# A graph-convolution and expert kernel: edge masks inside the degree stage, first chunk counted behind the degrees, h made two tiles at a time

## The chip, the cores and the metric

The kernel runs on one core of a Trainium2 chip. The metric is the device time of one execution in microseconds; runs of one kernel are compared by their median. Five engines work in parallel, each through its own instructions in order: TensorE (PE: matmuls, with weight loads shown as PEld), VectorE (DVE), ScalarE (ACT), GpSimd (POOL) and SyncE (SP), which only issues DMAs here. They wait for each other through semaphores.

## The reference, cut to what matters

The inputs are 6250 nodes with 256 features each and 200000 edges, `src[e]` to `dst[e]`, sorted by `dst`. The part in question is the graph convolution:

```python
deg_out = clip(segment_sum(ones, src), 1.0)
deg_in  = clip(segment_sum(ones, dst), 1.0)
h = feats * rsqrt(deg_out)[:, None]
m = segment_sum(h[src], dst) * rsqrt(deg_in)[:, None]
x = m @ W_gc + b_gc + (feats @ W_res + b_res)
```

Behind it come a top-2 mixture of 64 experts (`x @ Wg`, the two best experts of each node, a two-layer network per expert with GELU), a normalisation over the nodes, the sum with the input, and a layer norm over the features. The change touches none of these.

## The kernel before

The nodes lie in 50 tiles (`NT`) of 125. The edges lie in 1563 groups of 128, one edge per partition, one group per column of `dst` and `src` (padded to 1568 columns, `NGR`).

**Degree stage (lines 412 to 456).** A loop over 49 steps `i`, of 32 groups each (`CG`). In each step VectorE builds two one-hot tensors of `src`: `hot_hi` (its tile number, 50 values) and `hot_lo` (its place in the tile, 128 values), both at line 243. TensorE multiplies them group by group and so counts the out-degrees in `degp` (line 436). In the same step TensorE turns one tile of the features (line 383) and multiplies it by the two weight matrices (`project`, line 392); ScalarE copies the result (`hx`, line 396), and SyncE's queue carries one half to `r_dram` and the other into `hrow`, the rows of h in SBUF. From step 8 on GpSimd makes one `ind` tensor per step (line 428) that TensorE multiplies (`held`), and ScalarE makes the masks `mis` (line 456): for each group, how far each edge's `dst` lies from the start of its window.

**The gap behind it (lines 460 to 544).** VectorE sums the degrees, ScalarE takes the square root, VectorE the reciprocal (`s_out`). Then come the halves of h: each tile of `hrow` is scaled and split into a rounded half (ScalarE, line 488) and the remainder to it (line 491 on VectorE; for every third tile ScalarE makes the product `whole` and GpSimd subtracts, line 496). Every four or six tiles go to `h_dram` by SyncE's queue. Calls of `halves(0)` to `halves(40)`, ten tiles each, alternate with VectorE's mask steps: which edges of the first 1025 groups (`GD`) fit their window, which key each of them has (`key`, in f32), how many do not fit (`nmis`, `some`, `redo`), and a table `mf` of the edges left over, which GpSimd completes and writes to `mis_dram`.

**Aggregation (lines 551 to 827).** The first 1025 groups are "dense": 31 chunks, each a window of 128 destination nodes. For each group VectorE makes a one-hot `hotk` from `key` (line 615; every eighth group also `lo`, line 243), TensorE counts edges between source places and windows (line 625), and ScalarE copies the counts of one slot into `counts` (line 633), of which there are two, for even and odd chunks. Then `multiply(c, t)` multiplies the counts of chunk `c` by tile `t` of `hrow`, in two halves (lines 640 and 641), for 50 tiles. Chunk 0 has 20 slots of two groups, 40 counts. The counts of chunk `c + 1` lie between the tiles of chunk `c`; chunk 1 has 57 slots, 114 counts. `hot_of` runs seven groups ahead (`KB`). Before chunk 0 is counted, ScalarE clears `counts[0]` (five steps, line 595); it clears `counts[1]` between the counts of chunk 0. The remaining 538 groups are "gathered": GpSimd fetches the 128 source rows of a group from `h_dram` by an indirect DMA (line 567, a ring of six) and TensorE multiplies them by a one-hot of the window (lines 572 and 573).

The order of all this is written out by hand (`manual_schedule`): a generator `dense()` yields each piece of work with planned microseconds, and a gather is put in whenever the planned time passes `LEAD + n * every`, where `every` is chosen so that the last gather comes 5 planned microseconds before the end. The planned times are no durations; they only set the order. The plan gives 11.9 to the counting of chunk 0 and reaches 50.6 at its last tile.

Behind the aggregation come routing and the experts, unchanged.

## Time and profile before

| | us |
|---|---|
| median of three runs | 1770.24 (1765.89 to 1771.05) |
| the profiled execution | 1785.41 |
| its span | 1783.6 |
| TensorE busy in it | 1468.9 (82%) |
| VectorE busy | 1005.9 (56%) |
| GpSimd busy | 936.1 (52%) |
| ScalarE busy | 700.6 (39%) |
| mean granted TensorE clock | 0.929 of full speed |

The profile is one execution. Its times count from the start of its span. "Line, engine, operation, out<-in, shape, xcount" names an instruction or a merged run of equal ones; behind it in the timeline stands, in brackets, how long the engine was idle before and what released it; in a list of groups stand the busy time, the mean duration in ns, and the idle time before. A row by stretches gives the length, the busy time of TensorE, its weight loads, VectorE, ScalarE and GpSimd with their instruction counts, the granted clock, the DMA engines' busy share and the rate in GB/s. Starts and ends of matmuls are modelled in part, and a few of their records are missing. The degree stage lies between about 30 and 186 us, the aggregation between 227 and 1087, the experts behind 1180.

### The profile page before, as it was taken

The page shows a single profiled execution, that of the slowest core. Times are in us where ns is not written, and L with a number is a line of the kernel's source. Part 1 is how long each engine was busy: PE and PEld are TensorE (multiplying, and loading weights), DVE is VectorE, ACT ScalarE, POOL GpSimd, SP SyncE. Part 2 cuts the span into 40 slices and gives each one's busy share as a digit, 9 for nine tenths or more (in the row PEclk, how much of TensorE's full clock was granted, in tenths as well). Part 3 has the DMA queues.
Part 4 walks back from the last instruction along what each step waited for, and adds up shares of the span by engine and source line. Part 5 has one row for each costly group of instructions (what it writes and reads, how often), then busy time and mean ns, then how long its engine had stood idle before and what let it go on. Part 6 is the DMA issues. An engine that isn't in the chain of part 4 may idle for free. (4 is left out here: it accounts for less than half of the span.)

```text
span 1783.6 us, 31676 instructions
## 1 busy us (share of the span) xinstructions
PE 1468.9 (82%) x10293; PEld 1220.2 (68%) x10293; DVE 1005.9 (56%) x2588; ACT 700.6 (39%) x1703; POOL 936.1 (52%) x984
## 2 busy tenths in 40 slices
PE   5999168788899998999898896359999999999740
PEld 3555057677788888888888795248878887777520
DVE  8999886676666565545454551862322322221796
ACT  2333663333455554445444441032222222222248
POOL 3562436666666666666666664025655666554000
PEclk8999668999999999999999998579999999999875
DMA  5898766676777777677776773917878888675834
GB/s 169 245 257 243 237 179 180 194 196 190 206 214 195 199 213 209 186 211 205 201 206 199 215 205 109 223 48 225 265 221 246 251 248 255 202 252 183 222 88 127
DMA packets 221105, 362.19 MB, mean 203 GB/s; under 512 B 24820, under 2 KB 149614, under 8 KB 220930
## 3 DMA queue, kind: packets, MB, share of 16 engines
q1 hardware_dynamic: 158039, 180.12, 35.0%
q0 software_dynamic: 55328, 172.48, 34.4%
q10 hardware_dynamic: 7562, 7.47, 1.5%
q8 instruction: 84, 1.38, 0.3%
q14 instruction: 92, 0.75, 0.2%
HBM read 279.11 MB, written 74.47 MB: 198 GB/s over the span
## 5 line engine op out<-in xcount | busy, mean ns | idle before, releaser
L567 POOL DMA_INDIRECT r<-h_dram,srcg x538 | 556.6, 1035 | 301.5 <-issue 112.5
L640 PE MATMUL sm<-hrow,counts 125*128 125x258 f32 x1550 | 504.3, 341 | 8.6 <-issue 6.0
L633 ACT CAST counts<-pc 128x300 f32 (+7 forms) x804 | 356.3, 443 | 328.4 <-PE pc L625 160.3
L615 DVE TENSOR_SCALAR hotk<-iota_h,key 128x300 bf16<-128x300 f16 (+7 forms) x1025 | 274.2, 307 | 329.4 <-PE pc L625 169.3
L641 PE MATMUL sm<-hrow,counts 125*128 125x256 f32 x1550 | 418.9, 285 | 1.1 <-issue 1.1
L640 PEld LDWEIGHTS sm<-hrow,counts 125*128 125x128 f32 x1550 | 305.5, 197 | 76.1 <-issue 67.6
L625 PE MATMUL pc<-hotk,lo 128*128 128x300 bf16 (+7 forms) x1025 | 281.7, 302 | 85.6 <-issue 39.3
L641 PEld LDWEIGHTS sm<-hrow,counts 125*128 125x128 f32 x1550 | 302.3, 195 | 1.6 <-issue 1.0
L1262 ACT ACTIVATE hT<-ph,b1c 128x128 f32<-128x128 f32 (+8 forms) x256 | 109.2, 438 | 350.3 <-PE ph L1260 224.6
L1272 PE MATMUL py<-w2s,hT 128*128 128x256 f32 (+3 forms) x992 | 239.5, 384 | 4.6 <-issue 3.1
L1260 PE MATMUL ph<-xgT,w1s 128*128 128x128 f32 (+8 forms) x1024 | 211.8, 351 | 8.3 <-ACT hT L1262 4.1
L1260 PEld LDWEIGHTS ph<-xgT,w1s 128*128 128x128 f32 x1024 | 171.2, 193 | 41.7 <-issue 16.4
L1272 PEld LDWEIGHTS py<-w2s,hT 128*128 128x128 f32 (+3 forms) x992 | 165.4, 175 | 46.0 <-issue 7.8
L572 PE MATMUL pg<-r,hot 128*128 128x258 f32 x538 | 178.4, 332 | 19.1 <-issue 8.4
L1226 POOL DMA_INDIRECT y_dram<-ys,dest x124 | 119.2, 961 | 134.0 <-DVE ys L1275 63.1
L1226 POOL DMA_INDIRECT xg<-x_dram,ids x124 | 121.3, 978 | 110.6 <-DVE ids L1178 70.5
L573 PE MATMUL pg<-r,hot 128*128 128x256 f32 x538 | 152.9, 284 | 0.0
L1275 DVE TENSOR_TENSOR ys<-py,b2s 128x256 f32<-128x256 f32 (+3 forms) x124 | 51.7, 421 | 179.0 <-PE py L1272 118.8
L625 PEld LDWEIGHTS <-lo 128*128 128x128 bf16 x1025 | 90.0, 102 | 72.4 <-issue 26.3
L572 PEld LDWEIGHTS pg<-r,hot 128*128 128x128 f32 x538 | 104.7, 195 | 36.1 <-issue 17.9
L1250 DVE COPY xgT<-pte 128x256 f32<-128x256 f32 (+7 forms) x64 | 38.5, 601 | 160.9 <-PE pte L1248 69.9
L573 PEld LDWEIGHTS pg<-r,hot 128*128 128x128 f32 x538 | 104.4, 194 | 1.2 <-issue 0.4
(317 smaller groups left out, 1826.3 us busy)
## 6 DMA issues: line engine op xcount, KB each, us to landing
w1s<-in_L_gnn_w_dram SPq DMA_DIRECT2D x64, 512.0 KB
w2s<-in_L_gnn_w_dram SPq DMA_DIRECT2D x64, 512.0 KB
y_dram<-zeros SPq DMA_DIRECT2D x48, 256.0 KB
yr<-y_dram SPq DMA_DIRECT2D x25, 448.0 KB
r<-h_dram,srcg POOLq DMA_INDIRECT x538
b2s<-in_L_gnn_b_dram SPq DMA_DIRECT2D x64, 128.0 KB
h_dram<-hrow SPq DMA_DIRECT2D x5, 1344.0 KB
z_dram<-zeros ACTq DMA_DIRECT2D x7, 903.0 KB
```

Source lines behind the costliest of these rows:

```text
L567: G.indirect_dma_start(out=f32(r[:, :2 * D]), out_offset=None, in_=h_dram[:, :], in_offset=bass.IndirectOffsetOnAxis(ap=idx, axis=0))
L572: T.matmul(pg, hot, r[:, D:], start=first, stop=False)
L573: T.matmul(pg[:, :D], hot, r[:, :D], start=False, stop=last)
L615: V.tensor_scalar(hots[g], iota_h[:, :NT * w], key[:, g:g + 1], None, op0=ALU.is_equal)
L625: T.matmul(pc, los[g // PAIRS][:, r // 2, :, r % 2], hots.pop(g), start=(i == 0), stop=(i == k - 1))
L633: S.copy(counts[c % 2][:, :, ds(live["at"][j % 8], w)], pc.rearrange("p (t w) -> p t w", w=w))
L640: T.matmul(sm, by, hrow[:, t, D:], start=(t == 0), stop=False)
L641: T.matmul(sm[:, :D], by, hrow[:, t, :D], start=False, stop=(t == NT - 1))
L1226: w = G.indirect_dma_start(**kw)
L1260: T.matmul(ph[:, :m], w1s[:, kk, c * 128:(c + 1) * 128], xgT[:, kk, :m], start=(kk == 0), stop=(kk == 1))
L1262: S.activation(hT[:, c, :m], ph[:, :m], AF.Gelu, bias=b1_e[:, c:c + 1])
L1272: T.matmul(py[:n], hT[:, c, k * 128:k * 128 + n], w2s[:, c, :], start=(c == 0), stop=(c == 3))
```

## The change

The masks of the dense groups are made with fewer steps and inside the degree loop, at fixed steps `i` (the table `masks`): the difference to the window's start, that difference clipped, "clipped differs from unclipped" as the mark of an edge that does not fit, and the key. `wide` now holds the width less one for the clip, and is then overwritten by ScalarE with the tile number times the width. For the gathered groups ScalarE writes the distance straight into `keyg`, and two VectorE steps make their mask. ScalarE sums both marks with `accum_out`, and makes `mf` apart from its last sum, which GpSimd does at step 41 (`FIRST_IND + ND + 1`); the write of `mis_dram` follows at step 42. The `ind` tensors start at step 9. `away` gets a third row, one small VectorE step. A one-column square root at step 46 precedes the real one.

Behind the degrees, the first one-hots and the counts of chunk 0 follow at once. `halves(t)` now makes two tiles, `t - 1` and `t`: two rounded halves on ScalarE, the product of the second tile on VectorE, its subtraction on GpSimd, the remainder of the first on VectorE. One such pair follows every four counts of chunk 0 (ten pairs), the other fifteen come before every second tile of chunk 0's multiplication. The six first fetches and the first one-hots of the gathers (`first_rows`) follow the last pair; the sums over the misfits (`left_edges`) come at tile 45. `counts[1]` is filled with zeros by a DMA from the cleared `z_dram` on ScalarE's queue. `LEAD` goes from 30 to 50. The SBUF pools are put in another order, so that what is used last in the degree stage lies under what is used late in the aggregation.

```diff
-LEAD = 30.0
+LEAD = 50.0
...
+            following = lp.tile([128, NGR], F32, name="following", tag="dst")
+            hi = lp.tile([128, NGR], F32, name="hi", tag="b")
+            zeros = lp.tile([128, D + 2], F32, name="zeros")
+            unfit = lp.tile([128, GD], FP16, name="unfit")
+            fit = lp.tile([128, NGR - GD], FP16, name="fit")
+            kd = dp.tile([128, GD], FP16, name="kd")
+            kc = dp.tile([128, GD], FP16, name="kc")
+            past = dp.tile([128, NGR - GD], FP16, name="past")
...
-                    G.memset(wide[:, DENSE[a][0]:g0 + k * n], float(w))
+                    G.memset(wide[:, DENSE[a][0]:g0 + k * n], float(w - 1))
+                    wides.append((DENSE[a][0], g0 + k * n, w))
...
+            CG, FIRST_IND = 32, 9
...
+            masks = {
+                8: lambda: V.tensor_tensor(kd, dstf[:, :GD], key[:, :GD], ALU.subtract),
+                10: lambda: V.scalar_tensor_tensor(kc, kd, 0.0, upmost, op0=ALU.max, op1=ALU.min),
+                12: lambda: V.tensor_tensor(unfit, kc, kd, ALU.not_equal),
+                14: lambda: V.scalar_tensor_tensor(kd, unfit, -4096.0, kc, op0=ALU.mult, op1=ALU.add),
+                16: lambda: V.tensor_tensor(key[:, :GD], kd, wide, ALU.add),
+                18: lambda: S.activation(kd, unfit, AF.Copy, accum_out=nmis[:, 0:1]),
+                19: lambda: S.activation(mf[:, :GD], unfit, AF.Copy, scale=-4.0 * FAR, bias=4.0 * FAR),
+                25: lambda: V.tensor_scalar(past, keyg, 0.0, None, op0=ALU.is_ge),
+                26: lambda: V.scalar_tensor_tensor(fit, keyg, float(WIN), past, op0=ALU.is_lt, op1=ALU.mult),
+                28: lambda: S.activation(past, fit, AF.Copy, accum_out=nmis[:, 1:2]),
+                29: lambda: S.activation(mf[:, GD:], fit, AF.Copy, scale=FAR),
+                FIRST_IND + ND + 1: lambda: G.tensor_tensor(mf, mf, dstf, ALU.add),
+                FIRST_IND + ND + 2: lambda: G.dma_start(out=mis_dram, in_=mf),
+            }
+            off = [(S.activation, (keyg[:, g0 - GD:g0 - GD + k], dstf[:, g0:g0 + k], AF.Identity),
+                    neg[:, ND + c:ND + c + 1]) for c, (g0, k) in enumerate(GATHER)]
...
-                    V.scalar_tensor_tensor(upmost, following[:, :GD], 1.0, wide, op0=ALU.add, op1=ALU.min)
+                    V.scalar_tensor_tensor(upmost, following[:, :GD], 0.0, wide, op0=ALU.add, op1=ALU.min)
+                    for g, h, w in wides:
+                        S.activation(wide[:, g:h], hi_b[:, g:h], AF.Copy, scale=float(w))
...
-                if i >= 8:
-                    c = i - 8
+                if i in masks:
+                    masks[i]()
+                if i >= FIRST_IND:
+                    c = i - FIRST_IND
...
+                if i == 7:
+                    S.activation(keyg[:, NGU - GD:], dstf[:, NGU:], AF.Copy)
+                if i == 46:
+                    dsb = dp.tile([128, D], F32, name="dsb", tag="some")[:, :128]
+                    V.memset(dsb, 0.0)
+                    S.activation(kd[:, :1], ones[:, :1], AF.Sqrt)
...
-            V.tensor_tensor(kd, dstf[:, :GD], key[:, :GD], ALU.subtract)
...
-            S.activation(s_out, s_out, AF.Sqrt)
-            V.tensor_scalar(fit, mis, 0.0, None, op0=ALU.is_ge)
-            V.tensor_scalar(t1, mis, float(WIN), None, op0=ALU.is_lt)
-            V.reciprocal(s_out, s_out)
-
...
-            halves(0)
-            fd, td, wd = fit[:, :GD], t1[:, :GD], dp.tile([128, GD], FP16, name="wd")
-            V.tensor_mul(fit, fit, t1)
-            V.tensor_scalar(td, kd, 0.0, None, op0=ALU.is_ge)
-            V.tensor_mul(fd, fd, td)
-            V.tensor_tensor(wd, kd, upmost, ALU.subtract)
-            V.tensor_scalar(td, wd, 0.0, None, op0=ALU.is_lt)
-            halves(10)
-            V.tensor_mul(fd, fd, td)
-
-            V.scalar_tensor_tensor(t1, dstf, float(N), fit, op0=ALU.is_lt, op1=ALU.subtract)
-            mf = dp.tile([128, NGR], F32, name="mf", tag="b")
-            G.tensor_scalar(mf[:, :GD], t1[:, :GD], -4.0 * FAR, 4.0 * FAR, op0=ALU.mult, op1=ALU.add)
-            G.tensor_scalar(mf[:, GD:], t1[:, GD:], -FAR, FAR, op0=ALU.mult, op1=ALU.add)
-            G.tensor_tensor(mf, mf, dstf, ALU.add)
-            G.dma_start(out=mis_dram, in_=mf)
-            nmis = dp.tile([128, 1], F32, name="nmis")
-            V.tensor_reduce(nmis, t1, AX.X, ALU.max)
...
-            V.tensor_mul(wd, wide, hi_b[:, :GD])
-            V.tensor_add(kd, kd, wd)
-            V.tensor_scalar(kd, kd, BIG, None, op0=ALU.add)
-            halves(30)
-            V.tensor_mul(kd, kd, fd)
-            V.tensor_scalar(key[:, :GD], kd, BIG, None, op0=ALU.subtract)
-
-            V.tensor_copy(keyg, mis[:, GD:])
-            pn = ps_a.tile([1, 128], F32, name="pn", tag="pt")
-            T.transpose(pn, nmis, ident)
...
+            nc.scalar.dma_start(out=f32(counts[1]).rearrange("p t w -> p (t w)"),
+                                in_=z_dram[0:25 * 128, :].rearrange("(p r) d -> p (r d)", p=128)[:, :NT * WIN])
+            cleared(0, 0, 10)
+            cleared(0, 10, 10)
+            S.activation(s_out, s_out, AF.Sqrt)
+            for t0 in range(20, NT, 10):
                 cleared(0, t0, 10)
+
+            wholes = [t[:, u, :D] for t in (xs.tile([TP, 2, D + 2], F32, name="whole", tag="z"),
+                                            xs.tile([TP, 2, D], F32, name="whole2", tag="xr2")) for u in range(2)]
+
+            def halves(t):
+                for u in (t - 1, t):
+                    S.activation(hrow[:, u, :D], f32(hrow[:, u, D:2 * D]), AF.Copy, scale=s_out[:, u:u + 1])
+                whole = wholes[t // 2 % 4]
+                V.tensor_scalar(whole, f32(hrow[:, t, D:2 * D]), s_out[:, t:t + 1], None, op0=ALU.mult)
+                G.tensor_tensor(hrow[:, t, D:2 * D], whole, f32(hrow[:, t, :D]), ALU.subtract)
+                V.scalar_tensor_tensor(hrow[:, t - 1, D:2 * D], f32(hrow[:, t - 1, D:2 * D]), s_out[:, t - 1:t],
+                                       f32(hrow[:, t - 1, :D]), op0=ALU.mult, op1=ALU.subtract)
+                if t % 5 == 4 or t % 10 == 5:
+                    n = 6 if t % 10 == 5 else 4
+                    node_dma(nc.sync, False, f32(hrow[:, t + 1 - n:t + 1, :2 * D]), node_rows(h_dram, t + 1 - n, n))
+
+            def left_edges():
+
+                V.tensor_sub(nmis[:, 0:1], nmis[:, 0:1], nmis[:, 1:2])
...
-                    if c == 0 and j % 4 == 3 and j < 20:
-                        cleared(1, j // 4 * 10, 10)
...
+                V.reciprocal(s_out, s_out)
                 g, n = 0, DENSE[0][1] * DENSE[0][3]
+                made_of = 1
                 for g in range(n):
                     yield of_one_hots(0) / n, lambda g=g: count(g)
+                    if g % 4 == 3:
+                        yield 0.0, lambda t=made_of: halves(t)
+                        made_of += 2
...
+                        if c == 0 and t % 2 == 0 and made_of < NT:
+                            yield 0.0, lambda t=made_of: halves(t)
+                            made_of += 2
+                            if made_of > NT:
+                                yield 0.0, lambda: first_rows()
+                        if c == 0 and t == 45:
+                            yield 0.0, lambda: left_edges()
...
-            for n in range(NR):
-                fetch(ring[n], srcg[:, rows[n][1] - GD:rows[n][1] - GD + 1])
-            hot_rows(0)
+            def first_rows():
+                for n in range(NR):
+                    fetch(ring[n], srcg[:, rows[n][1] - GD:rows[n][1] - GD + 1])
+                hot_rows(0)
```

79 lines of the change are left out of this document (28 added, 51 removed).

## The prediction

> **What bounds the kernel now.** I read the page, then busy time stretch by stretch around the change, the waits, the timeline. The first count, first and last multiplication of chunk 0, and first gather are picked from TensorE's timeline; the stretches are cut there.
>
> ```profile
> 56.00:152.00 96.00, 96.00 (x1141) 56.58 (x1143) 94.26 (x62) 36.89 (x118) 62.96 (x29) 1.00 0.87 251
> 185.70:227.60 41.90, 0.40 (x2) 0.13 (x3) 37.05 (x64) 32.88 (x74) 20.31 (x33) 0.54 0.82 254
> 227.60:240.50 12.90, 6.23 (x40) 3.55 (x40) 10.91 (x52) 11.41 (x27) 0.00 (x0) 0.50 0.90 282
> 240.50:262.00 21.50, 19.22 (x135) 16.61 (x136) 18.02 (x78) 11.87 (x37) 9.10 (x8) 0.78 0.33 87
> 262.00:283.30 21.30, 17.16 (x111) 14.63 (x111) 14.30 (x56) 6.86 (x22) 14.47 (x14) 0.78 0.66 185
> 283.30:1077.70 794.40, 711.45 (x5255) 645.20 (x5255) 455.84 (x1510) 374.62 (x861) 529.35 (x513) 0.99 0.73 201
> 240.55 0.58 PE L640 MATMUL sm<-hrow,counts 125*128 125x258 f32 x1 [1.89 <-ACT counts L633]
> 283.27 0.42 PE L641 MATMUL sm<-hrow,counts 125*128 125x256 f32 x1
> ```
>
> Columns: stretch, length, then busy time of TensorE, its weight loads, VectorE, ScalarE, GpSimd; then the clock, DMA share and GB/s. In the degree stage (first row) TensorE and VectorE are both full. Then TensorE stands still for 41.9 us while VectorE (37.05) makes masks and halves of h. Counting chunk 0 takes 12.9 more. From 283.3 on TensorE is 90% busy (711.45 of 794.40), so its work sets the pace there. What the change can win lies between 180 and 283.3.
>
> **The change, part by part.** First, the masks that move into the degree loop.
>
> ```profile
> 106.61 1.11 PE L436 MATMUL degp<-hot_lo,hot_hi 128*50 128x128 bf16 x32
> 107.78 0.98 DVE L243 TENSOR_TENSOR hot_hi<-hi_b,iota 128x1600 bf16<-128x1600 bf16 x1
> 108.68 2.37 DVE L243 TENSOR_TENSOR hot_lo<-lo_b,iota 128x4096 bf16<-128x4096 bf16 x1
> 113.07 1.11 PE L436 MATMUL degp<-hot_lo,hot_hi 128*50 128x128 bf16 x32
> 151.85 0.21 DVE L371 CAST places<-pp 31x64 int32<-31x64 f32 x1 [1.68 <-PE pp L370]
> 177.88 2.27 DVE L243 TENSOR_TENSOR hot_lo<-lo_t,iota 128x4096 bf16<-128x4096 bf16 x1
> 180.74 1.11 PE L436 MATMUL degp<-hot_lo,hot_hi 128*50 128x128 bf16 x32
> 182.51 1.23 DVE L470 TENSOR_TENSOR kd<-dstf,key 128x1025 f16<-128x1025 f32 x1
> L480 DVE TENSOR_SCALAR fit<-mis 128x1568 f16<-128x1568 f16 x1 | 0.6, 559 | 0.0
> L505 DVE TENSOR_TENSOR fit<-fit,t 128x1025 f16<-128x1025 f16 x1 | 0.7, 697 | 0.0
> L511 DVE SCALAR_TENSOR_TENSOR t<-dstf,fit 128x1568 f16<-128x1568 f32 x1 | 1.8, 1793 | 0.0
> ```
>
> VectorE gets seven mask steps in the loop. The difference and the final key go through f32: 1.23 each, 2.46. Two fused steps over 1025 columns cost 1.79 x 1025/1568 = 1.17 each, 2.34; one over 543 columns 0.62. `not_equal` on 16-bit data 0.70 (the L505 row; 1.23 if it ran like kd). `is_ge` over 543 columns 0.3 (under the 0.56 for 1568). With one small step for `away` (0.2, like L371), 6.6 us.
>
> How much of this shows? VectorE issues hot_hi and hot_lo back to back, and hot_hi starts as the degree matmul two steps earlier ends (107.72 and 107.78): both engines are tight. VectorE's 1.68 us wait at L371 shrinks by about 1.0 when it is the later engine, and its lead over TensorE at the end (180.15 to 180.74) gives 0.6. So 5.0 remain. The whole lead inside the loop (the hot_lo that ends at 111.05 is used at 113.07, so 2.0) could be absorbed instead of the 0.6; then it is 3.6.
>
> Beside this, GpSimd's sum of mf moves from the gap to step 41 of the loop.
>
> ```profile
> 205.82 3.48 POOL L515 TENSOR_TENSOR mf<-mf,dstf 128x1568 f32<-128x1568 f32 x1
> 206.11 3.23 DVE L521 TENSOR_SCALAR okc<-okc,okd 128x31 f32<-128x31 f32 x1
> 214.94 0.84 POOL L496 TENSOR_TENSOR hrow<-whole,hrow 125x256 fp32r<-125x256 f32 x1 [0.20 <-ACT whole L495]
> 215.33 1.01 DVE L526 TENSOR_TENSOR kd<-kd,wd 128x1025 f16<-128x1025 f16 x1
> L491 DVE SCALAR_TENSOR_TENSOR hrow<-hrow,s_out 125x256 fp32r<-125x256 f32 x33 | 17.8, 595 | 2.4 <-ACT hrow L488 2.4
> L496 POOL TENSOR_TENSOR hrow<-whole,hrow 125x256 fp32r<-125x256 f32 x17 | 14.2, 836 | 51.7 <-ACT whole L495 50.4 <-DMA h_dram<-hrow 1.2
> 223.58 3.13 DVE L491 SCALAR_TENSOR_TENSOR hrow<-hrow,s_out 125x256 fp32r<-125x256 f32 x7
> ```
>
> A 31-column step of VectorE (L521) lasted 3.23 us and ended with GpSimd's L515: it was held. L526 (1.01 against 0.70 for L505) also ends one ordinary duration after GpSimd's 0.84 us subtraction. In the loop VectorE has only such 16-bit two-input steps, so mf costs 0 to 3.3; I take 3.0, by the L521 row. The degree stage thus ends 8.0 us later (3.6 to 9.9).
>
> Behind the degrees ScalarE is on the path.
>
> ```profile
> 164.78 0.43 ACTq L452 DMA_DIRECT2D z_dram<-zeros  x1
> 185.62 0.59 ACT L396 COPY hx<-pr 125x512 f32<-125x512 f32 x1 [1.13 <-PE pr L392]
> L479 ACT ACTIVATE s_out<-s_out 125x50 f32<-125x50 f32 x1 | 0.2, 245 | 0.0
> 223.70 3.59 ACT L595 ACTIVATE counts<-iota_f 128x1280 fp32r<-128x1280 f32 x3 [0.45 <-issue]
> 229.64 1.17 ACT L633 CAST counts<-pc 128x100 f32 x4
> L488 ACT ACTIVATE hrow<-hrow,s_out 125x256 fp32r<-125x256 f32 x50 | 21.6, 496 | 0.5 <-DVE s_out L482 0.5
> ```
>
> On the old time axis: hx done 186.2, one DMA issue 0.43, five clears of counts[0] at 1.20, Sqrt 0.24: 192.9. Two count copies at 0.29 and one half of h at 0.43 (21.6/50) later, at 193.9, VectorE has its first difference to make, done by 194.4. VectorE's seven first one-hots, and TensorE's first counts, lie before that.
>
> ```profile
> 17.54 0.91 DVE L154 TENSOR_SCALAR hi<-hi 128x1440 f32<-128x1440 f32 x1
> 229.69 1.32 DVE L615 TENSOR_SCALAR hotk<-iota_h,key 128x100 bf16<-128x100 f16 x8
> 270.16 1.68 DVE L615 TENSOR_SCALAR hotk<-iota_h,key 128x150 bf16<-128x150 f16 x8
> L243 DVE TENSOR_TENSOR lo<-lo_b,iota 128x1024 bf16<-128x1024 bf16 x9 | 6.1, 675 | 0.0
> 258.01 0.36 PE L572 MATMUL pg<-r,hot 128*128 128x258 f32 x1
> 258.33 0.24 PE L625 MATMUL pc<-hotk,lo 128*128 128x150 bf16 x1
> 192.25 45.15 SPq L165 DMA_DIRECT2D h_dram<-hrow  x20
> ```
>
> A round is four counts and one pair of tiles. VectorE: four one-hots at 0.165 (0.66), half a `lo` (0.34), and the pair. The pair is one product (0.27: between 0.16, scaled from L154, and 0.45), one fused step (3.13/7 = 0.45), and what GpSimd's subtraction takes from VectorE. For that: nothing in the 3.13 row, (17.8 - 33 x 0.45)/17 = 0.17 over all fused steps, 0.3 for L526, up to 0.84 if the whole operation were serial. I take 0.28, next to L526, since most steps here are of its kind: pair 1.0, round 2.0. ScalarE needs only 1.45 per round. Nine more rounds end at 212.4. So chunk 0 can be multiplied some 20 us earlier on the gap's side (240.5 against 212.4 + 8.0).
>
> Then 15 pairs remain, beside chunk 1's counts: until tile 28 VectorE makes 76 one-hots at 0.21 (16.0), 9.5 `lo` (6.4) and the pairs (15.0): 37.4, to 249.8. The last 21 tiles: 38 one-hots and five `lo`, 11.4, then seven tiles at some 0.43: 14.4; the old stretch 262 to 283.3, less eleven gathers at 0.32 (258.01 to 258.33), gives 17. I take 15: 264.8, with the 8.0 of the degree stage 272.8, against 283.5.
>
> That wins 10.7. But 18 gathers that ran before 283.3 (counted in the timeline) now come after: with LEAD 50 the plan starts them at the end of chunk 0. At 0.32 on a full TensorE, 5.8. **Sum: 4.9 us faster.**
>
> Costed at nothing: chunk 1's clearing by DMA (3.3 MB, 12 us at the 282 GB/s of the counting row; needed only after tile 1, some 25 us after its issue on ScalarE's queue; that queue's earlier writes are long out); late, it would hold the counts' copies. The ScalarE sums in the loop (ScalarE is 36.89 of 96 busy, and 31 small mask steps leave it). The mis_dram write, now on GpSimd's queue inside the loop (784 KB, 3 us of transfers, with the DMA at 0.87). `left_edges`: ten tiny steps at tile 45, where VectorE has no one-hots left; TensorE's transpose may wait 0.5. The six fetches, now behind the last pair on GpSimd's queue: h written by about 262 (pairs done at 257.8, plus a tenth of the 45.15 us), ten us before the first gather; without this cover they would hold that gather. SP's queue only gets the same h writes earlier.
>
> The profiled execution took 1785.41 us, its span 1783.6; the median of the runs is 1770.24, 0.85% less. 1785.4 - 4.9 = 1780.5, times 1770.24/1785.41: 1765.4 as a median.
>
> **The rivals.** *VectorE and GpSimd shut each other out* (the other side). If each subtraction costs VectorE its full 0.84, a pair is 1.56, and 24 pairs on the path add 13.4: 8.5 slower, 1778.7. It decides above a pair of 1.2. L521 and L526 speak for it, the 3.13 row (a subtraction ran under it) against. The Trainium skill (SBUF — State Buffer, "SBUF: two separate sides") states just this: VectorE's 2-port modes, or two SBUF inputs against a GpSimd operation that reads SBUF, hold one port pair exclusively. By that rule the time would be 1779; L521 agrees with it, the fused steps do not.
>
> *The cover is better*: the loop absorbs the masks (3.6 instead of 8.0, with mf in VectorE's gaps as the ind steps are: hot_lo 2.37 against 2.27) and pairs cost 0.72. Then 4.4 + 6.7 more: 16 us faster, 1754.5. The h write bounds it: 45 us of transfers cannot start before 197.
>
> *The counting does not move*:
>
> ```profile
> PE pc L625 <- DMA h_dram<-hrow: 17.6, 1, 17.6
> ```
>
> The first count is listed as released by a write of h. Were that real, only the 8.0 would remain: 1778. But VectorE's one-hot, its last pair of steps behind the halves, ends just before it; the wait reads better as VectorE's.
>
> **How the numbers follow.** About 0.3% (5.3 us) is what can be told from no change. Chances: forecast, 0 to 10 us faster, 0.45 (0.25 of it beyond 0.3%); better cover 0.20; port 0.25 (0.05 within 0.3%); no move or another wait 0.10 (0.03 within). Faster 0.45, same 0.28, slower 0.27. The range 1750 to 1780 takes in the better cover and the port case at its price; the forecast's own is 1760 to 1770.
>
> **What would show it.** Last degree matmul near 189 instead of 180.7; VectorE without idle from step 10 on; a long hot step of VectorE beside mf. First count near 195, the gap under 10 us. Chunk 0's first multiplication near 220, last near 273, no gather before it. VectorE over 90% busy from 200 to 258, a pair's steps near 1.0. From then on the same pace, some 0.6 gathers more per chunk. Wrong if: a pair costs over 1.2, the loop grows over 10, TensorE waits for counts[1] or for h, or the clock stays at half beyond chunk 0.

## The result, and the profile after

The changed kernel takes 1788.44 us (1783.80 to 1791.39) where the kernel before, run beside it, takes 1770.64 (1765.89 to 1773.54): a ratio of 1.0101, 95% interval 1.0068 to 1.0134. It is 17.8 us slower; 4.9 us faster was forecast, and the range ended at 1780.

The two profiles do not show this in their spans (1783.6 before, 1782.0 after): that of before comes from an execution 15 us above its median, that of after from the fastest one of its kernel. Chips differ too: the kernel before takes 1784, 1768 and 1664 us on three of those used below. So the pages are read here for the order of things, and times are compared only between runs on one chip. A trace is one execution too, and can lie some us above or below the median of its kernel; where that matters, it is said.

First, stretches of the changed kernel (degree stage, the gap before the first count, counting, chunk 0, the rest of the dense chunks), and last the rest in the kernel before. The end of chunk 0 and of the rest is the last matmul of the 50th tile of chunk 0 and of chunk 30, found by counting the multiplications. Columns as in the prediction: stretch, length, busy time of TensorE, its weight loads, VectorE, ScalarE, GpSimd, clock, DMA share, GB/s.

```profile
56.00:160.00 104.00, 99.60 (x1170) 58.70 (x1169) 100.11 (x66) 34.84 (x96) 88.90 (x30) 0.97 0.81 234
191.31:196.81 5.50, 3.83 (x10) 1.60 (x11) 3.03 (x14) 2.19 (x3) 0.00 (x0) 1.00 0.88 248
196.81:220.74 23.93, 7.47 (x41) 2.91 (x41) 19.28 (x68) 16.37 (x45) 6.46 (x21) 0.57 0.72 249
220.74:271.49 50.75, 41.30 (x219) 32.94 (x219) 49.51 (x177) 29.34 (x89) 19.22 (x22) 0.57 0.72 220
271.49:1096.88 825.39, 731.21 (x5401) 660.58 (x5400) 462.14 (x1530) 375.48 (x865) 544.69 (x534) 0.99 0.72 203
284.97:1098.59 813.62, 727.38 (x5366) 659.93 (x5364) 458.56 (x1524) 375.83 (x864) 532.03 (x515) 0.99 0.72 199
```

TensorE's timeline of the same kernel: the last degree matmul, the first count, the first multiplication, the first gather, the last multiplication of chunk 0.

```profile
190.17 1.12 PE L466 MATMUL degp<-hot_lo,hot_hi 128*50 128x128 bf16 x32
196.81 1.08 PE L625 MATMUL pc<-hotk,lo 128*128 128x100 bf16 x7 [1.68 <-issue]
220.74 0.58 PE L638 MATMUL sm<-hrow,counts 125*128 125x258 f32 x1 [2.66 <-ACT counts L633]
270.59 0.30 PE L535 MATMUL pg<-r,hot 128*128 128x258 f32 x1
271.21 0.28 PE L639 MATMUL sm<-hrow,counts 125*128 125x256 f32 x1
```

From the end of the last degree matmul to the first count it takes 5.5 us (191.29 to 196.81), where the kernel before took 45.7 (181.85 to 227.58; the prediction's 41.9 begins 4 us later, behind the last matmul of the degree sums). Up to here all is as forecast: first multiplication 220.74 (forecast 220.4), end of chunk 0 271.5 (272.8). In the kernel before chunk 0 ends at 285.0: the 283.27 that the prediction shows as its last multiplication is three tiles earlier, and its stretch up to 1077.7 ends 21 us ahead of the last multiplication of the dense chunks. Chunk 0 is thus done 13.5 us earlier than before. Then 825.4 us follow where the kernel before took 813.6, in an execution 15 us above its median. The loss lies there, where the change moves little but the places of the gathers.

What starts later is GpSimd's stream of fetches. The kernel before, from the timelines of SyncE and GpSimd: the writes of h (first issue, length from first to last), the first, seventh and last of the 538 fetches.

```profile
192.25 45.15 SPq L165 DMA_DIRECT2D h_dram<-hrow  x20
244.55 1.13 POOL L567 DMA_INDIRECT r<-h_dram,srcg  x1 [20.13 <-issue]
258.76 1.75 POOL L567 DMA_INDIRECT r<-h_dram,srcg  x1 [6.28 <-PE pc L625]
1081.49 1.01 POOL L567 DMA_INDIRECT r<-h_dram,srcg  x1 [0.49 <-PE sm L659]
```

The changed kernel, the same four:

```profile
210.87 48.52 SPq L165 DMA_DIRECT2D h_dram<-hrow  x20
264.71 1.27 POOL L530 DMA_INDIRECT r<-h_dram,srcg  x1 [6.16 <-DMA h_dram<-hrow]
273.20 0.95 POOL L530 DMA_INDIRECT r<-h_dram,srcg  x1 [0.30 <-issue]
1083.58 1.01 POOL L530 DMA_INDIRECT r<-h_dram,srcg  x1 [1.91 <-remote]
```

The first fetch comes 20.2 us later: the degree stage ends 9.4 later (180.74 to 190.17), from there to the first write of h it takes 9.2 more (11.5 to 20.7, since clears, counts and rounds of pairs now lie between), the writes take 3.4 longer, and the rest takes 1.8 less (7.1 to 5.3 from the last write's issue to the fetch). In the kernel before, the seventh fetch waited 6.28 us for the first gather to free a buffer of the ring; in the changed one nothing waits, so the seventh is 14.4 us later. This is the place to look.

### The profile page after: what moved, and what is told of

It reads as the page before. It is cut to its first block, busy times and chain, and to the rows that moved or that the text cites. A ratio compares the mean times of both kernels' runs of the same rounds, so it can differ in the third digit from the quotient of the medians.

```text
span 1782.0 us, 31709 instructions
## 1 busy us (share of the span) xinstructions
PE 1482.6 (83%) x10293; PEld 1222.6 (69%) x10293; DVE 1000.0 (56%) x2598; ACT 684.1 (38%) x1668; POOL 956.3 (54%) x991
## 5 line engine op out<-in xcount | busy, mean ns | idle before, releaser
L530 POOL DMA_INDIRECT r<-h_dram,srcg x538 | 550.3, 1023 | 275.8 <-issue 94.0
L615 DVE TENSOR_SCALAR hotk<-iota_h,key 128x300 bf16<-128x300 f16 (+7 forms) x1025 | 282.5, 313 | 328.4 <-PE pc L625 176.5
L625 PE MATMUL pc<-hotk,lo 128*128 128x300 bf16 (+7 forms) x1025 | 287.4, 307 | 77.0 <-issue 38.5
L1272 PEld LDWEIGHTS ph<-xgT,w1s 128*128 128x128 f32 x1024 | 170.5, 192 | 36.8 <-issue 14.2
L535 PEld LDWEIGHTS pg<-r,hot 128*128 128x128 f32 x538 | 103.4, 192 | 67.7 <-issue 28.9
L625 PEld LDWEIGHTS <-lo 128*128 128x128 bf16 x1025 | 90.1, 104 | 64.1 <-DVE hotk L615 18.2
L458 POOL TENSOR_SCALAR ind<-iota_f,pos 128x128 bf16<-128x128 f32 x31 | 87.7, 2834 | 43.2 <-PE held L460 41.4
```

The costliest lines, as they stand in the source:

```text
L530: G.indirect_dma_start(out=f32(r[:, :2 * D]), out_offset=None, in_=h_dram[:, :], in_offset=bass.IndirectOffsetOnAxis(ap=idx, axis=0))
L535: T.matmul(pg, hot, r[:, D:], start=first, stop=False)
L615: V.tensor_scalar(hots[g], iota_h[:, :NT * w], key[:, g:g + 1], None, op0=ALU.is_equal)
L625: T.matmul(pc, los[g // PAIRS][:, r // 2, :, r % 2], hots.pop(g), start=(i == 0), stop=(i == k - 1))
L1272: T.matmul(ph[:, :m], w1s[:, kk, c * 128:(c + 1) * 128], xgT[:, kk, :m], start=(kk == 0), stop=(kk == 1))
```

## The experiments

Two readings stood against each other at first. By the forecast, a gather costs 0.32 us of TensorE wherever it lies. By the other, called feeding, behind chunk 0 the fetches need their own time, and a gather that is put off costs about that.

**On one chip: both kernels again, and LEAD alone.** The kernel before and the changed kernel without an edit, the kernel before with the changed kernel's LEAD, and the changed kernel with a smaller one:

```diff
 e1_before_lead50
-LEAD = 30.0
+LEAD = 50.0
 e2_after_lead38
-LEAD = 50.0
+LEAD = 38.0
```

> The kernel before, unchanged, for its trace on the same chip as the others of this group. Both theories: the time of the kernel before, about 1770 us; chunk 0's last multiplication near 283, the aggregation's dense part done near 1065 to 1078.

> The changed kernel, unchanged, for its trace beside that of before on one chip. Theory G (the stretch behind chunk 0 gives the win back, because the 18 gathers that moved there cost more than 0.32 us each): chunk 0 ends 10 to 13 us earlier than in the kernel before, and the rest of the aggregation is 25 to 30 us longer. Theory D (the degree stage and the slow counting cost it): chunk 0 does not end earlier on the same chip, the rest is at most 8 us longer. Both: 15 to 20 us slower in all.

> The kernel before with LEAD 50 for 30 and nothing else: the gathers start at the end of chunk 0. Theory G: the loss comes from starting them late, so 10 to 25 us slower than before. Theory D: TensorE has the same work and no new wait, so within 4 us of before (18 gathers less in chunk 0 and 18 more behind it).

> The changed kernel with LEAD 38 for 50: gathers may start from about tile 30 of chunk 0, right behind the last pair of tiles and the first fetches. Theory G: 6 to 15 us faster than the changed kernel, since some ten gathers go back into chunk 0, unless TensorE then waits for h to be written. Theory D: within 3 us of the changed kernel.

Measured, against 1783.99 for the kernel before: the changed kernel 1800.86, ratio 1.0086 (1.0057 to 1.0116); before with LEAD 50 1800.08, 1.0086 (1.0055 to 1.0116); after with LEAD 38 1802.38, 1.0090 (1.0065 to 1.0114). The stretches "chunk 0", from its first multiplication to its last, and "the rest", from there to the last multiplication of the dense chunks; first the kernel before:

```profile
241.16:282.03 40.87, 35.75 (x254) 29.68 (x254) 33.13 (x137) 19.05 (x59) 23.86 (x22) 0.87 0.46 135
282.03:1093.79 811.76, 724.72 (x5365) 658.64 (x5364) 458.90 (x1524) 376.08 (x864) 527.26 (x517) 0.99 0.69 200
```

Before with LEAD 50:

```profile
241.50:275.98 34.48, 30.61 (x218) 25.12 (x218) 30.09 (x131) 18.68 (x58) 6.53 (x7) 0.84 0.16 48
275.98:1111.58 835.60, 737.32 (x5401) 664.15 (x5400) 465.04 (x1529) 376.44 (x865) 546.29 (x532) 0.99 0.69 199
```

The changed kernel:

```profile
222.05:272.05 50.00, 40.79 (x219) 31.63 (x219) 48.91 (x175) 29.34 (x89) 18.57 (x22) 0.59 0.72 223
272.05:1118.17 846.12, 741.67 (x5402) 669.25 (x5400) 463.93 (x1532) 375.00 (x865) 544.42 (x534) 0.98 0.68 198
```

The changed kernel with LEAD 38:

```profile
221.86:291.75 69.89, 46.04 (x240) 36.81 (x241) 52.40 (x181) 29.77 (x90) 31.09 (x35) 0.60 0.70 213
291.75:1111.90 820.15, 726.56 (x5380) 658.73 (x5378) 464.30 (x1525) 376.69 (x864) 538.43 (x521) 0.99 0.69 199
```

And its first gather, from TensorE's timeline:

```profile
269.19 0.58 PE L535 MATMUL pg<-r,hot 128*128 128x258 f32 x1 [9.20 <-DMA r<-h_dram,srcg]
```

LEAD 50 alone shows what was forecast and what was not. Chunk 0 gets 6.4 us shorter for the 18 gathers that leave it, 0.36 each, near the 0.32 of the prediction. Its first six fetches still begin at 244.4, but the seventh waits for the first gather, now at 275.1, to free a buffer, and the rest gets 23.8 longer, 1.3 for each (1.1 without the 4.5 us by which this trace lies above the median of its kernel). So a late start of the gathers alone makes the kernel before as slow as the changed one. And LEAD 38 cannot mend it: the first gather comes at 269.2 (with LEAD 50 at 271.2), because h is not there earlier. TensorE stands for it in chunk 0, which lasts 69.9 us instead of 50.0; the 11 gathers that now lie in it explain 4 of these 19.9. Yet the whole takes as long as with LEAD 50. Sixteen microseconds of TensorE's time were lost and cost nothing, so TensorE does not set the end.

Where the loss stands is told by TensorE's idle time just before the gathers (the number behind the second bar), over the rest: the kernel before, the same with LEAD 50, the changed kernel.

```profile
L572 PE MATMUL pg<-r,hot 128*128 128x258 f32 x519 | 170.9, 329 | 16.0 <-DMA r<-h_dram,srcg 7.0 <-issue 6.2 <-DVE hotk L615 1.3
L572 PE MATMUL pg<-r,hot 128*128 128x258 f32 x537 | 177.7, 331 | 36.3 <-issue 14.3 <-DMA r<-h_dram,srcg 12.8 <-DVE hot L790 5.2
L535 PE MATMUL pg<-r,hot 128*128 128x258 f32 x537 | 177.5, 331 | 34.1 <-DMA r<-h_dram,srcg 14.2 <-DVE hot L800 9.0 <-issue 8.4
```

It grows by 18 to 20 us, while the idle time before the counts (L625) stays at 58 to 60 us in all three.

**On another chip (1664.21 for the kernel before): half the fetches, a shorter ring, no mf.** The first two leave out every second fetch, so half of the gathered groups use whatever rows lie in their buffer; nodes then go to other experts, which take far longer, and only the aggregation of their profiles is read. The last one leaves out the sum `mf` and its write to `mis_dram`.

```diff
 f1_after_half_fetch, f2_before_half_fetch
-                if n + NR < len(rows):
+                if n + NR < len(rows) and n % 2 == 0:
 f3_after_ring5
-            NR = 6
+            NR = 5
 f4_after_no_mf
-                FIRST_IND + ND + 1: lambda: G.tensor_tensor(mf, mf, dstf, ALU.add),
-                FIRST_IND + ND + 2: lambda: G.dma_start(out=mis_dram, in_=mf),
```

> The changed kernel with every second fetch of source rows left out (the ring keeps the rows that lie there; half of the gathered rows are thus wrong ones), TensorE's work unchanged. Theory F (the gathers are fed at nearly their limit, so what is put off costs about 1 us each): 12 to 30 us faster than the changed kernel, the waits at the gathers' matmuls mostly gone. Theory P (a gather costs TensorE that much itself, wherever it lies): within 4 us of the changed kernel.

> The kernel before with the same fetches left out. Theory F: faster than before too, by 5 to 18 us, but by less than the changed kernel gains, so that the two stand within 8 us of each other. Theory P: within 4 us of before.

> The changed kernel with a ring of five fetched tiles in place of six. Theory F by the ring's depth (time from issue to landing): 8 us slower or more. Theory F by GpSimd's rate, and theory P: within 4 us of the changed kernel.

> The changed kernel without GpSimd's sum of mf at step 41 and the write of the left-over table behind it (both left out; the table isn't read when every edge fits). The prediction's term: the sum holds VectorE in the degree loop, so the degree stage ends 3.0 to 4.0 us earlier, the long hot_lo of 5.6 us is gone, and the kernel is 3 to 4 us faster. If TensorE's lag hides it: within 1.5 us.

The changed kernel with half the fetches, from the end of chunk 0:

```profile
272.87:959.82 686.95, 686.95 (x5401) 644.89 (x5400) 463.73 (x1530) 381.23 (x865) 274.08 (x268) 1.00 0.48 142
```

The kernel before with half the fetches:

```profile
275.14:957.55 682.41, 682.37 (x5366) 640.11 (x5364) 460.10 (x1523) 381.31 (x864) 263.68 (x257) 1.00 0.47 138
```

Now TensorE has no idle time (0.04 us at most), and the 18 put-off gathers cost 4.5 us, 0.25 each, no more than the prediction's price for TensorE. So 682 to 687 us is what TensorE needs on such a chip; with all fetches the kernel before (with smaller buffers) took 710.5 and the changed one 724.8 on one of the same speed (below). So fetching, not multiplying, makes the difference. This pair was run on a chip of this speed alone. Ring 5: 1697.24, ratio 1.0224 (1.0187 to 1.0260), far above the 1.0088 that the changed kernel has on such a chip: five buffers are too few here, as the reading by the time from issue to landing had forecast and the one by GpSimd's rate had not. Without mf: 1665.74, ratio 1.0015 (1.0001 to 1.0029). The degree stage ends 3.4 and 4.4 us earlier than in the two runs with mf on this chip (187.76 against 191.13 and 192.18, the last `degp` matmul). 3 to 4 us were forecast for the time as well, but against the 1.0088 of another chip it falls by some 12. This is not explained, and the traces do not settle it: this one lies 4.9 us above the median of its kernel, that of the other chip 6.6 below.

**On a chip at 1663.28: the control, an earlier start, a deeper ring.** To make room for a seventh buffer, two other buffers are made smaller, and a control has only this.

```diff
 g2_before_lead22
-LEAD = 30.0
+LEAD = 22.0
 g3_before_small_bufs, g4_before_ring7
-            KB = 7
+            KB = 6
-            HB = 4
+            HB = 3
 g4_before_ring7 alone
-            NR = 6
+            NR = 7
```

> The changed kernel once more, as the control of this chip. Feeding theory (a put-off gather costs about 1 us because each fetch needs its own time): first gather near 271, and the time stays 0.7 to 1.1% above the kernel before, 12 to 19 us. Full-TensorE theory (0.32 per put-off gather, the forecast): 5 us faster than before.

> The kernel before with LEAD 22 in place of 30, nothing else: the gathers begin some 9 us earlier (first one near 249 instead of 258), about five more of them lie inside chunk 0. Feeding theory: chunk 0 ends 2 us later (5 x 0.33), the rest is 5 to 7 us shorter, the whole 3 to 5 us faster. Full-TensorE theory: a gather costs 0.32 wherever it lies, within 1 us of before. Third possibility: h or the first fetches are not there at 249, TensorE stands in chunk 0 (as with LEAD 38 in the changed kernel), and the time is the same or a few us longer.

> Control for the next run: the kernel before with six instead of seven one-hots ahead (KB 6) and three instead of four windows per one-hot of the gathers (HB 3), ring still six. VectorE is 57% busy in the aggregation, so both theories expect within 0.3% (5 us) of before; HB 3 adds about 45 VectorE steps of a few tenths.

> The same with a ring of seven fetch buffers. Feeding theory by latency (a fetch takes a fixed time from issue to landing, the ring sets how many are under way): TensorE's waits at the gather matmul (16.0 us in the kernel before) shrink to under 8 and the time falls by 5 to 15 us against the control. Feeding theory by GpSimd's rate (1.0 us of GpSimd per fetch plus a gap): a deeper ring changes nothing beyond 0.3%. Full-TensorE theory: no change.

Measured: the changed kernel 1675.89, ratio 1.0088 (1.0059 to 1.0118); LEAD 22 1669.41, 1.0025 (1.0004 to 1.0046); small buffers 1665.91, 1.0021 (1.0004 to 1.0038); ring 7 1654.76, 0.9946 (0.9926 to 0.9966). The kernel before with seven buffers beats both kernels on this chip, by 0.5%; it was not run on a slower chip. Against its control that is 11.2 us: 5 to 15 were expected if the time to landing sets the pace, nothing beyond 0.3% if GpSimd's rate alone does. GpSimd's groups in the dense stretch tell how the fetches run (busy time, mean ns of one, idle before); the control first:

```profile
L567 POOL DMA_INDIRECT r<-h_dram,srcg x517 | 523.7, 1013 | 175.0 <-PE pc L625 70.0 <-issue 35.4 <-PE sm L641 29.6
```

The changed kernel's timeline of GpSimd on this chip:

```profile
323.88 0.95 POOL L530 DMA_INDIRECT r<-h_dram,srcg  x1 [0.30 <-PE sm L639]
325.13 0.95 POOL L530 DMA_INDIRECT r<-h_dram,srcg  x1 [0.30 <-PE pc L625]
326.39 0.98 POOL L530 DMA_INDIRECT r<-h_dram,srcg  x1 [0.30 <-PE pc L625]
327.68 0.95 POOL L530 DMA_INDIRECT r<-h_dram,srcg  x1 [0.30 <-PE pc L625]
```

GpSimd fetches nearly without a pause. Each fetch is 0.95 us or more, and before most there is the same 0.30, whatever releaser is named: 1.25 from start to start. Of 509 intervals between 300 and 980 us, 79% are under 1.4 us, and the mean of all is 1.336. The group says it too: (523.7 + 175.0) / 517 = 1.35. The page calls GpSimd 75% busy, since it does not count the 0.30. TensorE alone, by the rows with half the fetches, needs 686.95 / 537 = 1.28 per gather in the changed kernel, with all that lies around it, and 682.41 / 519 = 1.31 in the kernel before; GpSimd gives 1.34 and 1.35.

Whether GpSimd waits for TensorE can be read from the two timelines together: the buffer of a fetch is free once the gather six places earlier is done. On this chip it had been free for 1.2 us in the median when its fetch began (0.9 in the control, between 300 and 960 us), and 13% of the fetches (29%) began within 0.5 us of it. So now and then TensorE holds GpSimd up, the two paces lie close together, and a buffer more or less counts. On the chip at 1784 the buffer had been free for 2.9 to 3.2 us in three kernels, and under 2% of the fetches began within 0.5 us: there TensorE hardly ever holds the stream of fetches up once it runs.

LEAD 22 was forecast by the feeding theory as 3 to 5 us faster and is not: its seventh fetch came 3.2 us earlier than the control's (253.13 against 256.31), but its 531 fetches behind that took 727.5 instead of 717.6, and chunk 0 lasted 44.3 us instead of 36.3, more than its seven further gathers explain. That is the third possibility of the expectation, TensorE standing in chunk 0; why it was not made good later, as with LEAD 38, is not settled.

**On a chip at 1767.67: the deeper ring on the changed kernel, h made sooner, mf on VectorE, all three.**

```diff
 h1_after_ring7: KB 6, HB 3, NR 7 as above
 h2_after_h_early
-LEAD = 50.0
+LEAD = 28.0
-                    if g % 4 == 3:
+                    if g % 2 == 1:
                         yield 0.0, lambda t=made_of: halves(t)
 h3_after_mf_dve
-                FIRST_IND + ND + 1: lambda: G.tensor_tensor(mf, mf, dstf, ALU.add),
+                FIRST_IND + ND + 1: lambda: V.tensor_tensor(mf, mf, dstf, ALU.add),
 h4_after_all_three: all of these
```

> The changed kernel with seven fetch buffers (KB 6 and HB 3 make room, which cost 0.2% in the kernel before). If the loss behind chunk 0 is all feeding: at least the 0.7% that the deeper ring gave the kernel before, so a ratio of 1.000 to 1.003 to the kernel before, and the stage behind chunk 0 shorter by 8 to 12 us. If the loss is something else (work on VectorE or ScalarE, memory layout): it stays at 1.006 to 1.010.

> The changed kernel with one pair of halves behind every two counts of chunk 0 instead of every four (20 pairs there, five in the multiplication), and LEAD 28. Late-start theory: chunk 0's first multiplication moves from 222 to about 232 (ten pairs at 1.0 us of VectorE), the first gather from 271 to 247 to 252, some 15 to 20 gathers lie inside chunk 0, which ends at 275 to 280, and the time falls from 0.9% above the kernel before to 0.3% below up to 0.3% above it. If the start of the gathers does not matter: chunk 0 ends later by as much as its gathers cost, the time stays at 1.006 or worse. If VectorE is the limit: first multiplication behind 238 and no gain.

> The changed kernel with the sum mf at step 41 on VectorE (1568 columns in f32, some 1.9 us by the row of kd) instead of GpSimd. Forecast of the prediction (mf on GpSimd takes 3.0 from the degree stage): the stage ends about 1 us earlier. By the trace (4.0 us on GpSimd and a hot_lo of 5.60 beside it, where one takes 2.3): 1.4 to 2 us earlier. With all feeding-bound behind chunk 0 the time moves by under 2 us, ratio to the kernel before 1.007 to 1.009.

> The three edits together (h early with LEAD 28, mf on VectorE, ring of seven). Late-start theory: the gains add, 0.5 to 1.2% faster than the kernel before (8 to 20 us on a chip where that takes 1664). Without it: no better than the ring alone, 1.000 to 1.003.

Measured: ring 7 1785.33, ratio 1.0086 (1.0059 to 1.0112); h sooner 1781.57, 1.0059 (1.0037 to 1.0081); mf on VectorE 1780.98, 1.0071 (1.0050 to 1.0092); all three 1777.63, 1.0054 (1.0030 to 1.0078). A deeper ring does not take the loss away here. By its expectation that spoke for something else than feeding; but a stream that finds its buffers free (3.0 us in the median here too, with mf on VectorE) gains nothing by one more. TensorE's idle time before the gathers did fall (14.5 us against 36.8 with mf on VectorE), that before the counts rose (65.5 against 47.9); whether the two smaller buffers did that is not known, since they had no control on this chip. Making h sooner and all three together were expected to gain more (0.3% below to 0.3% above the kernel before, and 0.5 to 1.2% below it). With h sooner the first gather was to come at 247 to 252; it came at 265.4. The writes of h and the first fetch of that kernel, from the timelines of SyncE and GpSimd:

```profile
211.26 43.28 SPq L165 DMA_DIRECT2D h_dram<-hrow  x20
261.76 1.07 POOL L530 DMA_INDIRECT r<-h_dram,srcg  x1 [14.84 <-DMA h_dram<-hrow]
```

Its chunk 0:

```profile
229.50:301.00 71.50, 44.27 (x258) 35.89 (x259) 47.89 (x175) 22.55 (x71) 33.58 (x35) 0.71 0.71 208
```

The pairs were made twice as fast, but the writes of h still begin at 211 and take 43 us; only 5 us are won (48.5 to 43.3), and GpSimd waits for them. Again TensorE lost time in chunk 0 (71.5 us, against 50.0 in the run with mf on VectorE; its 20 further gathers explain 7 of the 21.5), and again the kernel is no slower for it: against that run its chunk 0 ends 29.5 us later (301.0 against 271.5) and its dense part 1.1 us earlier (1097.5 against 1098.5).

**On a chip at 1665.39: half of each row.** The count of the fetches stays; each brings 1 KB per row instead of 2 KB, and zeros stand for the remainder. The index is doubled (the sum of `srcg` with itself), since `h_dram` is now seen as two rows per node.

```diff
+                G.memset(f32(r[:, D:2 * D]), 0.0)
...
-                G.indirect_dma_start(out=f32(r[:, :2 * D]), out_offset=None, in_=h_dram[:, :],
+                G.indirect_dma_start(out=f32(r[:, :D]), out_offset=None, in_=h_dram[:, :].rearrange("n (k d) -> (n k) d", k=2),
...
+            G.tensor_tensor(srcg, srcg, srcg, ALU.add)
```

> The kernel before with fetches of 1 KB instead of 2 KB per row: only the rounded half of h is fetched for the gathered groups, the remainder is left out (zeros stand in its place, so the result is that of rounded rows there). Number of fetches, rows and GpSimd instructions as before. Bytes theory (a fetch moves 256 KB, at 1.5 us each 175 GB/s): the pace falls towards what the stage took with half the fetches (670 us for 538 on the faster chip, 1.25 each), the time is 1.5 to 5% shorter. Rate theory (GpSimd needs 1.03 us per fetch and waits for room in its queue, whatever the width): the pace stays, the time is within 0.5% of before.

> The changed kernel with the same half rows (the remainder left out likewise). If the pace of the gathers by their bytes ate the gain: now 0 to 5 us faster than the run with the kernel before and half rows, as the prediction's sum had it. If it is GpSimd's rate: 0.6 to 1.0% slower than that run, as with whole rows. If the loss is elsewhere: also slower by 0.6% or more though the pace has fallen.

Measured: before with half rows 1661.99, ratio 0.9983 (0.9963 to 1.0002); after with half rows 1671.17, 1.0038 (1.0017 to 1.0059), 9.2 us above the former. GpSimd's fetches in the dense stretch of the kernel before with half rows:

```profile
L569 POOL DMA_INDIRECT r<-h_dram,srcg x513 | 528.8, 1031 | 160.9 <-PE pc L627 59.5 <-issue 31.7 <-PE pg L575 28.8
```

And TensorE's largest wait in the changed kernel, first with whole rows (chip at 1663), then with half rows:

```profile
PE pg L535 <- DMA r<-h_dram,srcg: 21.3, 35, 1.8
PE pg L538 <- DMA r<-h_dram,srcg: 21.6, 36, 1.2
```

Half the bytes hardly change anything: 1031 ns per fetch against 1013, (528.8 + 160.9) / 513 = 1.34 per fetch against 1.35, and TensorE waits at the gathers 21.6 us, as with whole rows (21.3). The changed kernel is still 9.2 us (0.55%) behind, where it was 12.6 with whole rows on the other chip of this speed, and where 0.6 to 1.0% was expected. The bytes theory falls on this chip, a pace per fetch stands. The Trainium skill (Perfetto Trace Analysis, "What "DMA-bound" means") names a case like this: the issuing engine's track is solid DMA slices, and their length is the making of descriptors, not the moving of data. The trace agrees in the second (1031 ns against 1013 for twice the bytes); the slices are not quite solid, with 0.30 us between them. Its advice of larger descriptors was not tried; halving them changed the time by 0.2%.

**All together.** The seventh fetch is the first that needs a used buffer (the eighth with a ring of seven, the sixth with a ring of five); from it to the last are 531. Times from GpSimd's timelines, in us. The last column tells how far the traced execution lies above the median of its kernel:

| run | seventh fetch | last fetch | per fetch | ratio to before | trace above median |
|---|---|---|---|---|---|
| chip at 1784: before | 258.99 | 1079.31 | 1.545 | 1 | 0.3 |
| after, LEAD 38 | 273.42 | 1097.42 | 1.552 | 1.0090 | -5.5 |
| after | 274.87 | 1101.29 | 1.556 | 1.0086 | 4.5 |
| before, LEAD 50 | 275.77 | 1097.86 | 1.548 | 1.0086 | 4.5 |
| chip at 1768: after, all three | 266.33 | 1078.93 | 1.530 | 1.0054 | -2.2 |
| after, h sooner | 269.44 | 1083.77 | 1.534 | 1.0059 | 2.8 |
| after, mf on VectorE | 274.12 | 1085.28 | 1.528 | 1.0071 | 2.6 |
| after, ring 7 | 276.14 | 1084.75 | 1.523 | 1.0086 | 3.0 |
| chips at 1664: before, ring 7 | 252.74 | 970.12 | 1.351 | 0.9946 | 3.9 |
| before, LEAD 22 | 253.13 | 980.67 | 1.370 | 1.0025 | 1.0 |
| before, small buffers | 256.31 | 973.89 | 1.351 | 1.0021 | -2.9 |
| before, half rows | 257.09 | 970.17 | 1.343 | 0.9983 | -1.0 |
| after, without mf | 270.81 | 984.89 | 1.345 | 1.0015 | 4.9 |
| after, ring 5 | 273.96 | 1001.09 | 1.369 | 1.0224 | -7.6 |
| after | 274.12 | 983.74 | 1.336 | 1.0088 | -6.6 |
| after, half rows | 276.13 | 984.97 | 1.335 | 1.0038 | 2.5 |

On the two slower chips the pace per fetch hardly moves, whatever is done around it, and the time follows the seventh fetch: three different kernels that reach it at 273 to 276 all take 0.9% more, and the four of the second chip are in the order of their seventh fetch, though their intervals overlap. On the faster chips the later start is given back in part (10 to 15 us of 18 to 19 remain at the last fetch, with whole and with half rows), and LEAD 22, the ring of five and the run without mf do not follow the rule.

## Why the prediction was wrong

**Degree stage, 8.0 later (3.6 to 9.9).** It ended 9.4 later between the two pages, and 11.2 later between the two kernels on one chip (179.83 and 191.00). The parts, in the timeline of the changed kernel:

```profile
56.76 11.82 POOL L458 TENSOR_SCALAR ind<-iota_f,pos 128x128 bf16<-128x128 f32 x3 [27.38 <-PE held L460]
67.49 0.19 PE L460 MATMUL held<-ones_b,ind 128*128 128x1 bf16 x1 [4.26 <-POOL ind L458]
157.50 4.00 POOL L426 TENSOR_TENSOR mf<-mf,dstf 128x1568 f32<-128x1568 f32 x1
158.06 5.60 DVE L243 TENSOR_TENSOR hot_lo<-lo_t,iota 128x4096 bf16<-128x4096 bf16 x1
164.12 0.27 PE L381 MATMUL pp<-ident,away 128*31 128x128 f32 x1 [3.03 <-DVE away L379]
```

mf was priced at 3.0 and cost 3.4 to 4.4 by the run without it. `hot_lo` began 0.56 us after mf, could go on only when mf ended, and took 5.60 where it takes 2.30 alone; the port rule that the prediction cited (the Trainium skill, SBUF — State Buffer, "SBUF: two separate sides") lets the later one wait for the whole of the earlier, and the row agrees: 161.50 - 158.06 = 3.4 of waiting, and 2.2 of its own. On VectorE the same sum takes 1.8, and the degree stage ended 0.7 and 2.1 us earlier than in two runs with it on GpSimd (about 1 by the prediction's price and 1.4 to 2 by the trace were expected):

```profile
165.72 1.77 DVE L426 TENSOR_TENSOR mf<-mf,dstf 128x1568 f32<-128x1568 f32 x1
```

Not foreseen was the 4.26: beside VectorE's added steps GpSimd's `ind` steps stretch (three took 11.82, and the mean of all 31 went from 2107 to 2834 ns), and TensorE waits for one. The prediction had costed VectorE's added work only on VectorE. The mask steps themselves took about what was priced (1.22 for a fused one, 0.69 for `not_equal`), but TensorE's only long waits in the loop are the 4.26 for `ind` and the 3.03 behind mf's `hot_lo`; for a one-hot it waited 0.2. So the 5.0 that were to show of the masks do not show as such, and that 8.0 came near 9.4 is in part luck.

**ScalarE's chain, rounds of 2.0, pairs of 1.0.** Right: first count 196.81 (near 195), first multiplication 220.74 (220.4).

**Fifteen pairs, then a tail of 15; chunk 0 ends at 272.8.** Right: 271.5, no gather before it but one. The 283.5 that it was set against is really 285.0.

**"18 gathers ... at 0.32 on a full TensorE, 5.8".** This is the step that failed. Its premise, "TensorE is 90% busy ..., so its work sets the pace there", was read from one row by stretches, and the 83 us of idle time in that row were not asked for their cause. The 0.32 was right as a price on TensorE (0.36 with LEAD 50 alone, 0.25 with half the fetches), but the pace is that of GpSimd's fetches, 1.34 to 1.55 us each: a stream that starts later ends later. LEAD 50 alone measured 23.8 for 18 put-off gathers, 1.3 each. With 17.8 in place of 4.9 in the other direction, the sum missed by 22.7 us. The win of 10.7 in chunk 0 (it was 13.5) is off the path, and so it counts for nothing: TensorE reaches the gathers earlier and waits there.

**What then makes the time.** Not the gathers' place in the plan alone, as LEAD 38 showed, but what the prediction wrote under better cover: the h write takes 45 us and cannot start before h. It was used there as a bound on a gain, not as the head of a chain. That chain runs from the degree stage (9.4 later) through the first pairs of h (9.2 more) and the write of h (3.4 more) to the first fetch. The six first fetches were put at nothing, since h would be written ten us before the first gather. It was (259.4 against 270.6), but the fetches behind them follow at their own pace, and so the late first one counts. By this the degree stage's 8.0, which the sum set against a win elsewhere, would go to the end nearly whole; no run shows that part by itself.

**The rivals.** VectorE and GpSimd did shut each other out, but in the degree loop, and not in the pairs, where the time held. Better cover: no. The counting did move. None of the three named a late first fetch, and all of them took TensorE for the bound behind chunk 0. Among the signs of being wrong stood a TensorE that waits for h; it was GpSimd that waited for it (6.16 us).

## What to carry to other kernels

Judge an engine by the distance from one start to the next, not by its busy share: GpSimd at 66 to 75% was the slower stream, with 79% of its intervals on the faster chip at their shortest, and TensorE, at 90% or more, was not. Before pricing work that is put off at its cost on one engine, find the stream that it belongs to, that stream's own pace, and what its first item waits for; if the stream has no slack, its delay is the whole price. A step that makes idle time disappear gains only if it lies on the chain that ends last, and taking away time elsewhere (LEAD 38 and h made sooner both stopped TensorE for some 15 us, and the end did not move) is a cheap way to find out.

## What the runs showed of the hardware that was not expected

- An indirect DMA of 128 rows costs GpSimd 0.95 us at least and 0.30 before the next, with rows of 1 KB as with rows of 2 KB. On the slower chips the shortest interval is the same 1.25, but only 57 to 60% of the intervals are under 1.4 (79% on a faster one), and the mean is 1.52 to 1.56. There the longer ones come from idle time: over 0.35 us before 111 of 424 fetches of the changed kernel on the chip at 1784, against 16 of 495 on the chip at 1663. What holds GpSimd then is not shown.
- Fetches of over 1.00 us lie beside VectorE steps that read two tensors (L243, L800): in the changed kernel on a faster chip these fill 0.42 us of the first 0.95 in the mean, and 0.15 in shorter fetches. No run took these steps away.
- The same kernel took 1664 to 1784 us on different chips at nearly the same mean granted clock (0.92 to 0.94); in the rest behind chunk 0 the kernel before took 811.8 us on a slower one, and 710.5 with small buffers on a faster one. Why is not known.
- A ring of five instead of six fetch buffers cost 1.3% (1.0224 against 1.0088 on chips of one speed); a seventh gained 0.7% against its control on a faster chip, while on a slower one the changed kernel with it showed the same 1.0086 that the changed kernel had elsewhere.
- Small GpSimd steps took longer in the degree loop with VectorE's added steps: 2834 ns in the mean for a tensor of 128 x 128, against 2107. VectorE was 98% busy there before the change too (94.26 of 96.00), so that its load alone does it is not shown.
